# Two count matrices written in the order of the edges, the attention weights of layer 1 as the larger of 1 and a product

## The chip, the cores and the metric

The kernel runs on one core of a Trainium2 chip. Its engines are TensorE (PE, with its weight loads shown as PEld), VectorE (DVE), ScalarE (ACT), GpSimd (POOL) and SyncE (SP, which here only issues transfers). Six runs of the kernel before took 5446.58 to 5467.45 us, median 5455.3 us. The time is the device time of one execution in microseconds; lower is better.

## The reference, cut to what matters

A graph of N = 3125 nodes with 256 features and E = 50000 edges, sorted by `dst`, goes through four graph layers, each followed by a sum with its input and a layer norm. Layer 0 is a two-stage attention with a feed-forward part, layer 1 an attention with four heads, layer 2 two convolutions that sum over the edges and back, layer 3 a message product. The change is about layer 1 and about two matrices that layers 1 and 2 read:

```python
x  = h @ W                      # 3125 x 64
el = x @ Wl.T; er = x @ Wr.T    # 3125 x 4 heads
e  = exp(leaky_relu(el[src] + er[dst], 0.2))
w  = e / max(segment_sum(e, src), 1e-12)[src]
out[head] = segment_sum(w[:, head] * x[dst], src)
```

The kernel does not gather for layer 1. It writes a dense matrix `mats[0]`, in which row `dst`, column `src` holds how many edges lead from `src` to `dst`, and goes through all pairs: weight of a pair = count times exp(leaky_relu(el + er)). With the slope 0.2, exp(leaky_relu(z)) = exp(0.2 z) * exp(0.8 max(z, 0)); the factor exp(0.2 z) splits into a factor of the source and one of the target and is taken outside. `mats[1]` is the same matrix with rows and columns exchanged. Layer 2 reads both.

## The kernel before, in words

Nodes are padded to NP = 3200 = 25 tiles of 128 (`NN` = 25), edges to 50048 = 391 columns of 128 (`NT` = 391). The input `src` and `dst` come as 128 x 391 arrays whose column j holds the edges 128 j to 128 j + 127.

**Preparation** (`prepare`, L1991). The first projection, the query, key and value rows of layer 0, and the weights of layer 3's edges (`edge_weights`, L1890). `counts` (L1061) finds for each edge how many of the next edges are the same pair (`more`) and whether the same pair came before (`seen`); it works with partition p holding the edges 391 p to 391 p + 390, from an earlier copy of the edges in memory. It makes `count` (what is to be written), `put0` and `put1` (where in `mats[0]` and `mats[1]`); an edge whose pair came before, or a padding edge, is sent to a place behind the matrix. `put_by` and `fetch_by` carry such arrays through memory past a branch that chooses the path for sorted edges.

**Layer 0** (`attend`, L1405, called for l = 0 and l = 1) goes tile by tile over 25 tiles of 128 target nodes. Each tile's edges lie in a run of S = 17 columns of 128 slots. GpSimd gathers the key and value rows of the 17 columns with 17 indirect transfers (`fetch`, in three parts of 6, 6 and 5), then one more (`mine`) for the row sums' maxima. TensorE makes scores and sums, and the feed-forward of a group of three tiles (`feed`, L1302) is pumped in between. In `attend` every GpSimd and SyncE instruction is kept in program order (`InOrder`, L981). GpSimd's order in a tile is: 6 gathers of the next tile, fills, `mine`, then the next tile's other 11 gathers.

**Fills.** One fill is an indirect transfer of 128 counts of 2 bytes to 128 places of a matrix. `fill` (L1126) places it after a given transfer of GpSimd; L1487 puts FILL = 11 fills of `mats[0]` into each of the 25 tiles of l = 0, and L1620 the remaining 116 behind the last tile of l = 0. The fills of one matrix are declared independent of each other; a reader of the matrix waits for all of them. Cleared rows of `mats[1]` are also written in l = 0.

**Layer 1** (`layer1`, L1683). Three column blocks of 1280, 1280 and 640 sources (RS = 1280), each in two halves of two heads, each with 25 steps, one per tile of targets: 150 steps. A step loads a 128 x 1280 piece `m` of `mats[0]` (L1742, four buffers). For each of two heads it makes relu(el + er) (three times in five on VectorE, L1749, else on ScalarE, L1747), its exponential on ScalarE (L1751), the product with the counts on VectorE (L1752), and multiplies it into `acc` on TensorE (L1755). Each of the first 131 steps ends with `fill_slowly` (L1136): SyncE loads 3 columns of `put1` into a small tile (L1139, two buffers), and GpSimd makes three fills of `mats[1]` (L1142). SyncE's queue is strictly in order: the load of `put` for a step waits until a buffer is free, and the `m` of a later step stands behind it.

**Layers 2 and 3** read both matrices by blocks (`conv`, L1789), then gather rows of 1 KB (L91) for the last layer.

Of the kernel before, what the change touches and what calls it, by code (L numbers as in the profile page):

```python
# [57 lines left out]
FILL, FILL1 = 11, 3  # L58
# [943 lines left out]
class Sorted(General):  # L1002
# [58 lines left out]
    def counts(self, k, cp, sp, raw):  # L1061
# [6 lines left out]
        self.put1 = self.dram.tile([P, NT], I32, name="put1d")  # L1068
# [24 lines left out]
        nc.vector.tensor_copy(self.count, more)  # L1093
        d, src, code = (v[:, HALO:HALO + NT] for v in (d, src, code))
# [4 lines left out]
        nc.vector.tensor_max(away, away, pad)  # L1099
        behind = cp.tile([P, NT], F32, name="behind")  # L1100
        nc.gpsimd.iota(behind, pattern=[[1, NT]], base=NP * NP, channel_multiplier=NT,
                       allow_small_or_imprecise_dtypes=True)
        back = cp.tile([P, NT], F32, name="back")
        nc.vector.scalar_tensor_tensor(back, src, float(NP), d, op0=ALU.mult, op1=ALU.add)
        put1 = cp.tile([P, NT], I32, name="put1s")
        for c, to in ((code, self.put0), (back, put1)):
            gap = sp.tile([P, NT], F32, name="gap")
            nc.vector.tensor_sub(gap, behind, c)
            nc.vector.tensor_mul(gap, gap, away)
            nc.vector.tensor_add(to, gap, c)  # L1110
        nc.sync.dma_start(self.put1, put1)
# [8 lines left out]
    def zeros(self):  # L1120
        z = self.keep.tile([P, ZB], BF16, name="zmat")
        self.nc.vector.memset(z, 0.0)
        self.mats = [self.dram.tile([NP * NP + EP, 1], BF16, name=f"mat{i}") for i in range(2)]
        return z

    def fill(self, i, put, j, behind):  # L1126
# [6 lines left out]
        tc.declare_no_dep(ins.ins, group=f"fill{i}", reason="each place is written once")  # L1133
        tc.add_to_no_dep_group(f"fill{i}", ins.ins)

    def fill_slowly(self, i, sp, j0, j1):  # L1136

        put = sp.tile([P, FILL1], I32, name="put1")
        ins = self.nc.sync.dma_start(put[:, :j1 - j0], self.put1[:, j0:j1])  # L1139
        self.tc.keep_in_program_order(ins)  # L1140
        for j in range(j0, j1):
            ins = self.nc.gpsimd.indirect_dma_start(  # L1142
                out=self.mats[i], out_offset=bass.IndirectOffsetOnAxis(ap=put[:, j - j0:j - j0 + 1], axis=0),
                in_=self.count[:, j:j + 1], in_offset=None)
            self.tc.declare_no_dep(ins.ins, group=f"fill{i}", reason="each place is written once")
            self.tc.add_to_no_dep_group(f"fill{i}", ins.ins)
# [258 lines left out]
    def attend(self, l, qw):  # L1405
# [6 lines left out]
        with ExitStack() as at:  # L1412
# [48 lines left out]
            def scores(t):  # L1461
# [25 lines left out]
                for c in range(t * FILL, (t + 1) * FILL if l == 0 else 0):  # L1487
# [100 lines left out]
            for t in range(NN + 2):  # L1588
# [31 lines left out]
                for c in range(NN * FILL, NT if l == 0 and t == NN else 0):  # L1620
# [62 lines left out]
    def layer1(self, parts):  # L1683

        nc, tc, a = self.nc, self.tc, self.a
        A1 = D1 + 1
        mat = self.mats[0][:NP * NP, :].rearrange("(d s) o -> d (s o)", s=NP)
        with ExitStack() as at:  # L1690
# [14 lines left out]
            nc.vector.tensor_copy(wlb, l1.wr[:, H1:, None].to_broadcast([D1, H1, P]))  # L1705
            nc.scalar.activation(fe, er, AF.Exp, scale=0.2)
# [5 lines left out]
            def scores(s0, h0):  # L1712

                el = lp.tile([P, 2, RS], F32, name="el")
                for h in range(2):
                    for c in range(s0, min(s0 + RS, NP), 512):
# [3 lines left out]
                        nc.scalar.copy(el[:, h, c - s0:c - s0 + n], e_p[:, :n])  # L1720
# [4 lines left out]
            fills = iter(range(0, NT, FILL1))  # L1725
            for s0 in range(0, NP, RS):
                R = min(RS, NP - s0)
                ot = op.tile([A1, H1, RS], F32, name="ot")
                for h0 in range(0, H1, 2):
# [6 lines left out]
                    for t in range(NN):  # L1736
# [5 lines left out]
                        nc.sync.dma_start(m[:, :R], mat[t * P:(t + 1) * P, s0:s0 + R])  # L1742
                        for h in (h0, h0 + 1):
                            e = ep.tile([P, RS], F32, name="e")
                            z = er[:, t, h:h + 1]
                            if (2 * t + h) % 5 in (1, 3):
                                nc.scalar.activation(e[:, :R], el[:, h - h0, :R], AF.Relu, bias=z)  # L1747
                            else:
                                nc.vector.tensor_scalar(e[:, :R], el[:, h - h0, :R], z, 0.0,  # L1749
                                                        op0=ALU.add, op1=ALU.max)  # L1750
                            nc.scalar.activation(e[:, :R], e[:, :R], AF.Exp, scale=0.8)  # L1751
# [461 lines left out]
```

## Time and profile before

| | |
|---|---|
| median of six runs | 5455.3 us |
| profiled execution, its time / its span | 5455.55 us / 5453.7 us |
| busy: PE / DVE / ACT / POOL | 3957.5 / 2731.3 / 1436.7 / 2241.3 us |
| preparation | 0 to 285 us |
| layer 0, l = 0 | 285 to about 1873 us |
| layer 0, l = 1 | about 1873 to 2922 us |
| layer 1 | 2922 to 3613 us |
| layer 2 | 3613 to 4523 us |
| layer 3 | 4523 to 5454 us |
| fills in l = 0 (L1130) | 391, mean 976 ns |
| fills in layer 1 (L1142) | 391, mean 1252 ns |

The profile is of one execution. A busy time is the time in which an engine had an instruction under way; what lies between is idle time, put down to what ended it. "issue" is time in which the engine waited for nothing that the profile shows, "remote" a wait ended by something that it can't name. In a windows view each row is a stretch of the span in microseconds, its length, then for each engine the busy time and in brackets how many instructions began there, then the granted TensorE clock (1.00 is full), the share of the DMA engines and GB/s.

### The profile page before, as it was taken

How to read it: one execution, taken by the hardware profiler on the slowest of the kernel's cores; microseconds unless marked ns; L12 is line 12 of the kernel's file. 1: busy time of each engine (PE TensorE's matmuls, PEld its weight loads, DVE VectorE, ACT ScalarE, POOL GpSimd, SP SyncE). 2: the span in 40 equal slices, each digit the busy share in tenths (PEclk: the TensorE clock that was granted, in tenths of full speed). 3: DMA queues.
4: the chain of work that ended last, by engine and by line, in shares of the span. 5: the costliest groups of instructions: out<-in, count | busy, mean ns of one | idle time of the engine just before them, and what ended most of it. 6: DMA issues, size and time to landing. Idle time of an engine off the chain costs nothing.

```text
span 5453.7 us, 54504 instructions
## 1 busy us (share of the span) xinstructions
PE 3957.5 (73%) x18909; PEld 2660.9 (49%) x18909; DVE 2731.3 (50%) x5301; ACT 1436.7 (26%) x2460; POOL 2241.3 (41%) x2116
## 2 busy tenths in 40 slices
PE   6843656555555357777779989789999994777787
PEld 3432434344343245555564333346556553766677
DVE  7934535454453156666665888751221232444444
ACT  4600112111111002221225787765211110000000
POOL 0055544545456454454434878610000005455552
PEclk8866867777777668887888999899999996888878
DMA  8554534444330254555433222123333332122221
GB/s 192 145 180 120 151 106 134 137 132 138 100 115 21 93 162 147 154 168 146 146 118 81 68 61 68 41 76 89 92 104 87 100 111 76 58 68 68 70 70 38
DMA packets 381015, 577.19 MB, mean 106 GB/s; under 512 B 104265, under 2 KB 284100, under 8 KB 380669
## 3 DMA queue, kind: packets, MB, share of 16 engines
q1 hardware_dynamic: 264906, 286.55, 19.2%
q0 software_dynamic: 115824, 287.06, 18.1%
q8 instruction: 152, 2.49, 0.2%
q14 instruction: 133, 1.09, 0.1%
HBM read 486.46 MB, written 86.91 MB: 105 GB/s over the span
## 4 chain that ended last, share of the span: by engine, by line
PE 45%; another core or an unknown queue 17%; DVE 13%; issue 7%; POOL 5%; DMA 3%; ACT 2%; SPq 0%; DVEq 0%; ACTq 0%; POOLq 0%
PE cv L1806 9%; PE acc L1967 5%; PE acc L1547 5%; PE cv L1808 4%; PE acc L1755 4%; PE acc L1964 4%; PE qe L1471 3%; PE mm L1329 3%; POOL mat L1142 2%; PE mm L1343 2%; POOL kv L995 2%; DVE ws L1962 2%; DVE kv L1545 1%; DVE oh L1047 1%
## 5 line engine op out<-in xcount | busy, mean ns | idle before, releaser
L995 POOL DMA_INDIRECT kv<-kv,k_src x850 | 855.8, 1007 | 771.2 <-issue 232.7
L91 POOL DMA_INDIRECT g<-l_tab,k_src x425 | 445.6, 1048 | 1363.3 <-issue 1089.3
L1471 PE MATMUL qe<-q,oht 128*128 128x256 bf16 x2550 | 425.1, 317 | 550.0 <-DVE kv L1473 379.2
L1473 DVE TENSOR_TENSOR kv<-kv,qe 128x512 f32<-128x512 f32 (+1 forms) x450 | 289.3, 654 | 806.8 <-remote 509.8
L1471 PEld LDWEIGHTS <-oht 128*128 128x128 bf16 x2550 | 331.0, 148 | 655.5 <-issue 580.6
L1755 PE MATMUL acc<-e,xe 128*65 128x512 f32 (+2 forms) x1600 | 577.6, 517 | 67.0 <-DVE e L1752 45.3
L1142 POOL DMA_INDIRECT mat<-k_count,put x391 | 489.5, 1252 | 245.3 <-DMA put<-put1d 130.5
L1962 DVE TENSOR_TENSOR ws<-oh,w_n 128x512 f32<-128x512 f32 x425 | 290.4, 691 | 430.7 <-PE acc L1967 277.7
L1964 PE MATMUL acc<-g,ws 128*128 128x256 f32 x850 | 319.6, 463 | 216.6 <-DVE ws L1962 161.5
L1547 PE MATMUL acc<-kv,oh 128*128 128x264 f32 x1700 | 434.7, 413 | 33.5 <-DVE kv L1545 32.6
L1130 POOL DMA_INDIRECT mat<-k_count,k_put x391 | 381.5, 976 | 119.1 <-issue 119.1
L1967 PEld LDWEIGHTS acc<-g,ws 128*128 128x128 f32 x2550 | 411.0, 220 | 34.1
L1755 PEld LDWEIGHTS acc<-e,xe 128*65 128x65 f32 x1600 | 215.5, 142 | 421.9 <-issue 315.2
L1806 PE MATMUL cv<-parts,m 128*128 128x512 bf16 x1250 | 413.0, 381 | 7.5 <-DMA m<-mat 7.2
L1806 PE MATMUL cv<-mids,m 128*128 128x512 bf16 x1250 | 408.4, 379 | 10.7 <-DVE y L1828 9.5
L1967 PE MATMUL acc<-g,ws 128*128 128x128 f32 x2550 | 406.8, 303 | 0.0
L1547 PEld LDWEIGHTS acc<-kv,oh 128*128 128x128 f32 x1700 | 343.3, 206 | 109.9 <-DVE kv L1545 45.1
L1752 DVE TENSOR_TENSOR e<-e,m 128x1280 f32<-128x1280 f32 (+1 forms) x300 | 369.4, 1264 | 46.8 <-DMA m<-mat 25.5
L1806 PEld LDWEIGHTS <-m 128*128 128x128 bf16 x2500 | 245.0, 98 | 295.0 <-DMA m<-mat 9.3
L1808 PE MATMUL cv<-parts,m 128*128 128x256 bf16 x1250 | 339.2, 274 | 0.0
L1808 PE MATMUL cv<-mids,m 128*128 128x256 bf16 x1250 | 338.8, 273 | 0.0
L1751 ACT ACTIVATE e<-e 128x1280 f32<-128x1280 f32 (+1 forms) x300 | 317.5, 1087 | 66.0 <-DVE e L1749 47.7
(285 smaller groups left out, 5696.5 us busy)
## 6 DMA issues: line engine op xcount, KB each, us to landing
m<-mat SPq DMA_DIRECT2D x550, 160.0 KB
mat<-zmat SPq DMA_DIRECT2D x40, 1000.0 KB
m<-mat SPq DMA_DIRECT2D x100, 320.0 KB
keys<-e_dst SPq DMA_DIRECT2D x50, 544.0 KB
q<-q SPq DMA_DIRECT2D x100, 192.0 KB
kv<-kv,k_src POOLq DMA_INDIRECT x850
kv<-qkv SPq DMA_DIRECT2D x50, 256.0 KB
g<-l_tab,k_src POOLq DMA_INDIRECT x425
```

The lines of the kernel that those rows point to most:

```text
L91: return self.nc.gpsimd.indirect_dma_start(out=out, out_offset=None, in_=table, in_offset=bass.IndirectOffsetOnAxis(ap=idx, axis=0))
L995: ins = of(*args, **kw)
L1130: ins = tc.nc.gpsimd.indirect_dma_start(out=self.mats[i], out_offset=bass.IndirectOffsetOnAxis(ap=put, axis=0), in_=self.count[:, j:j + 1] ...
L1142: ins = self.nc.gpsimd.indirect_dma_start(out=self.mats[i], out_offset=bass.IndirectOffsetOnAxis(ap=put[:, j - j0:j - j0 + 1], axis=0), in ...
L1471: nc.tensor.matmul(qe[:, u, :], s.slots[:, h0 + s0 + u, :], s.q[:, k, :], start=(k == 0), stop=(k == 2))
L1547: nc.tensor.matmul(s.acc, s.oh[i][:, u, :], kv[:, u, D:], start=(h0 + u == 0), stop=(h0 + u == S - 1))
L1755: nc.tensor.matmul(accs[h, c][:, :n], xe[:, t, h, :], e[:, c:c + n], start=(t == 0), stop=(t == NN - 1))
L1806: nc.tensor.matmul(accs[i], block, parts[:, b, :2, :].rearrange("p a f -> p (a f)"), start=(b == 0), stop=False)
L1808: nc.tensor.matmul(accs[i][:, :D], block, parts[:, b, 2, :], start=False, stop=(b == NN - 1))
L1962: nc.vector.tensor_tensor(ws, oh[:, s, None, :].to_broadcast([P, 4, P]), w4[:, t, s, :, None].to_broadcast([P, 4, P]), op=ALU.mult)
L1964: nc.tensor.matmul(acc0, ws[:, 0, :], g[:, s, :], start=(s == 0), stop=(s == S - 1))
L1967: nc.tensor.matmul(acc1[:, m], ws[:, 1 + m, :], gb[:, 0:m + 2:m + 1, :], start=(s == 0 and m == 0), stop=(s == S - 1 and m == 2))
```

## The change

**Edge order.** `counts` now ends by writing one array `numbers` to memory: the count for an edge that is the first of its pair and real, else zero. A new function `places`, called after `edge_weights`, reads it back so that column j holds the edges 128 j to 128 j + 127 (four transposes on TensorE), loads `dst` and `src` as they come in, and makes `put0` and `put1` in that order; both also go to memory (`puts`). An edge with a zero count is sent behind the matrix.

**Exact dependences.** Since edges are sorted by target and 17 columns hold all edges of a tile's run, rows t of `mats[0]` are complete when its fills 0 to 17 (t + 1) - 1 have come. `filled` declares readers and fills independent of each other, and `row_of_counts` gives the load of `m` in step t of the first 25 steps just these fills to wait for.

**Where the fills go.** `mats[0]`: 3 in each tile of l = 0 and 50 behind its last tile, 2 in each tile of l = 1 and 130 behind its last tile (305 in all), and the last 86 in layer 1, 6 per step. `mats[1]`: 391 in layer 1 after them, 5 per step. There are 15 + 79 = 94 steps with fills.

**Weights.** With z = el + er, exp(0.8 max(z, 0)) = max(1, exp(0.8 el) exp(0.8 er)) = 1 + relu(exp(0.8 el) exp(0.8 er) - 1). `el` is stored as its exponential already (the copy from PSUM becomes an Exp), `fr` holds the target's factor, both shifted by `mid` to keep them in range. A step's head is then one ScalarE instruction (relu of factor times `el` minus 1) and one VectorE instruction (plus 1, times counts).

```diff
-FILL, FILL1 = 11, 3
+FILL = 3, 2
+FILLED = 0, 125, 305
+FILL0, FILL1 = 6, 5
...
-        nc.vector.tensor_copy(self.count, more)
...
+        nc.vector.tensor_mul(away, away, more)
+        nc.vector.tensor_sub(pad, more, away)
+        nc.sync.dma_start(self.numbers, pad)
+
+    def places(self, cp, rp):
+        n = cp.tile([P, LCH, P], F32, name="n_rows")
+        rows = self.numbers.rearrange("p j -> (p j)").rearrange("(r e) -> r e", e=P)
+        tp = rp.tile([P, 4, P], F32, name="rad_p")
+        for c in range(LCH):
+            m = min(P, NT - c * P)
+            nc.sync.dma_start(n[:m, c, :], rows[c * P:c * P + m, :])
+            nc.tensor.transpose(tp[:, c, :m], n[:m, c, :], self.ident[:m, :m])
+        num = tp.rearrange("p c e -> p (c e)")[:, :NT]
+        nc.vector.tensor_copy(self.count, num)
+        nc.vector.tensor_scalar(real, num, 0.0, None, op0=ALU.is_gt)
...
+        for (u, v), to in ((ends, self.put0), (ends[::-1], put1)):
+            gap = cp.tile([P, NT], F32, name="gap")
+            nc.vector.scalar_tensor_tensor(gap, u, float(NP), v, op0=ALU.mult, op1=ALU.add)
+            nc.vector.tensor_sub(gap, gap, behind)
+            nc.vector.tensor_mul(gap, gap, real)
+            nc.vector.tensor_add(to, gap, behind)
+        nc.sync.dma_start(self.puts[0], self.put0)
+        nc.sync.dma_start(self.puts[1], put1)
...
+    def filled(self, i, ins):
+        for g in (f"fill{i}", f"read{i}"):
+            self.tc.declare_no_dep(ins, group=g, reason="each place is written once")
+        self.tc.add_to_no_dep_group(f"fill{i}", ins)
+        self.fills[i].append(ins)
+
+    def row_of_counts(self, t, ins):
+        self.tc.declare_no_dep(ins, group="fill0", keep=self.fills[0][:S * (t + 1)],
+                               reason="the edges of this row have come")
...
-                for c in range(t * FILL, (t + 1) * FILL if l == 0 else 0):
+                for c in range(FILLED[l] + t * FILL[l], FILLED[l] + (t + 1) * FILL[l]):
                     self.fill(0, self.put0[:, c:c + 1], c, behind)
...
-                for c in range(NN * FILL, NT if l == 0 and t == NN else 0):
+                for c in range(FILLED[l] + NN * FILL[l], FILLED[l + 1] if t == NN else 0):
                     self.fill(0, self.put0[:, c:c + 1], c, behind_all[0])
...
-                        nc.scalar.copy(el[:, h, c - s0:c - s0 + n], e_p[:, :n])
+                        nc.scalar.activation(el[:, h, c - s0:c - s0 + n], e_p[:, :n], AF.Exp, scale=0.8,
+                                             bias=low[:, h0 + h:h0 + h + 1])
...
-            fills = iter(range(0, NT, FILL1))
+            fills = [(0, j, FILL0) for j in range(FILLED[2], NT, FILL0)] + [(1, j, FILL1) for j in range(0, NT, FILL1)]
+            fills = iter(fills)
...
-                        nc.sync.dma_start(m[:, :R], mat[t * P:(t + 1) * P, s0:s0 + R])
+                        ins = nc.sync.dma_start(m[:, :R], mat[t * P:(t + 1) * P, s0:s0 + R])
+                        if s0 == h0 == 0:
+                            self.row_of_counts(t, ins.ins)
                         for h in (h0, h0 + 1):
                             e = ep.tile([P, RS], F32, name="e")
-                            z = er[:, t, h:h + 1]
-                            if (2 * t + h) % 5 in (1, 3):
-                                nc.scalar.activation(e[:, :R], el[:, h - h0, :R], AF.Relu, bias=z)
-                            else:
-                                nc.vector.tensor_scalar(e[:, :R], el[:, h - h0, :R], z, 0.0,
-                                                        op0=ALU.add, op1=ALU.max)
-                            nc.scalar.activation(e[:, :R], e[:, :R], AF.Exp, scale=0.8)
-                            nc.vector.tensor_mul(e[:, :R], e[:, :R], m[:, :R])
+                            nc.scalar.activation(e[:, :R], el[:, h - h0, :R], AF.Relu, scale=fr[:, t, h:h + 1],
+                                                 bias=ones)
+                            nc.vector.scalar_tensor_tensor(e[:, :R], e[:, :R], 1.0, m[:, :R],
+                                                           op0=ALU.add, op1=ALU.mult)
...
-                        j = next(fills, None)
-                        if j is not None:
-                            self.fill_slowly(1, sp, j, min(j + FILL1, NT))
+                        for i, j, n in islice(fills, 1):
+                            self.fill_slowly(i, sp, j, min(j + n, NT))
...
             self.edge_weights(cp, rs, rp, *ew)
+            self.places(cp, rp)
             self.put_by()
```

Before the first step of layer 1 the changed kernel also finds `mid`, 0.4 times the difference between the largest `el` and the largest `er` of each head: a maximum over nodes, a transpose, another maximum, a small product on TensorE and four Exp instructions for `fr` (`fr`, `mid`, `low` in `layer1`). `fill_slowly` is as before, but loads from `puts[i]` a tile of up to six columns.

## Prediction

> **What bounds the kernel now.** I read the stages by windows, then the waits within a stage, then single instructions. No engine is busy throughout, so each stage has its own limit. The first two rows are the tile loops of layer 0, l = 0 and l = 1 (24 tiles between the first and the last `mine`), the next two are what follows the last `mine` in each.
>
> ```profile
> 339.50:1669.10 1329.60, 716.82 (x3400) 530.50 (x3399) 629.69 (x1223) 217.62 (x398) 685.02 (x690) 0.72 0.44 126
> 1919.90:2834.80 914.90, 645.05 (x3338) 506.39 (x3336) 591.04 (x1136) 189.90 (x351) 445.81 (x426) 0.81 0.52 154
> 1669.10:1873.00 203.90, 86.81 (x294) 57.74 (x293) 44.60 (x104) 29.17 (x64) 117.29 (x117) 0.71 0.07 19
> 2834.80:2927.20 92.40, 79.08 (x316) 57.11 (x316) 37.38 (x88) 32.96 (x70) 0.94 (x1) 0.82 0.20 53
> ```
>
> A tile takes 1329.6/24 = 55.4 us with 11 fills and 914.9/24 = 38.1 us without. In both, TensorE and VectorE do about the same work: 3.0 us more of TensorE and 1.6 us more of VectorE per tile at l = 0. The tails differ in the same way, 203.9 with 116 fills against 92.4 us. So fills cost time here though nothing in the tile loop reads them. The timeline shows how: VectorE stands for 65 and 41 us on a sum from TensorE, and GpSimd, done with its fills, waits another 51 us for the rows that this work makes.
>
> ```profile
> 1789.65 0.42 DVE L1347 TENSOR_TENSOR hs<-hs,mm 128x256 f32<-128x256 f32 x1 [65.38 <-remote]
> ...
> 1831.64 0.42 DVE L1347 TENSOR_TENSOR hs<-hs,mm 128x256 f32<-128x256 f32 x1 [40.90 <-remote]
> ```
> ```profile
> 1820.85 0.95 POOL L1130 DMA_INDIRECT mat<-k_count,k_put  x1 [0.30 <-issue]
> 1873.10 0.99 POOL L995 DMA_INDIRECT kv<-kv,k_src  x1 [51.29 <-DMA kv<-qkv]
> ```
>
> Why TensorE is slow beside a run of fills the profile does not say; I use the price only.
>
> Layer 1 is another matter. There fills run beside a TensorE that is nearly always busy (118.15 of 120 us, clock 1.00):
>
> ```profile
> 3300.00:3420.00 120.00, 118.15 (x330) 44.13 (x327) 101.88 (x86) 95.40 (x86) 96.53 (x75) 1.00 0.28 70
> 3480.00:3571.00 91.00, 66.78 (x225) 27.93 (x224) 57.12 (x85) 54.81 (x78) 69.71 (x64) 0.95 0.21 50
> ```
>
> The first row is 25 full steps with 75 fills: 4.8 us a step. A fill there takes 96.53/75 = 1.29 us and 0.30 us pass before the next, so three need 4.76 us: GpSimd is as full as TensorE. The second row is half-size steps: 64 fills of 1.09 us, again GpSimd's pace. After the last fill the half-size steps are shorter: 53 products, 26.5 steps, in 91 us (3.4 us a step) before, 32 products in some 40 us (2.5 us) after:
>
> ```profile
> 3480.00:3571.00 91.00, 42.67 (x53) 0.95 0.21 50
> 3571.00:3613.60 42.60, 25.27 (x32) 0.94 0.26 73
> ```
>
> The groups of layer 1 (count, busy, mean ns; then the idle time before):
>
> ```profile
> L1142 POOL DMA_INDIRECT mat<-k_count,put x391 | 489.5, 1252 | 245.3 <-DMA put<-put1d 130.5 <-issue 114.8
> L1752 DVE TENSOR_TENSOR e<-e,m 128x1280 f32<-128x1280 f32 x200 | 289.4, 1485 | 17.8 <-issue 9.0 <-ACT e L1751 5.7 <-DMA m<-mat 2.7
> L1751 ACT ACTIVATE e<-e 128x1280 f32<-128x1280 f32 x200 | 246.5, 1264 | 30.9 <-DVE e L1749 18.5 <-issue 11.3
> ...
> L1747 ACT ACTIVATE e<-el,er 128x1280 f32<-128x1280 f32 x80 | 108.5, 1356 | 57.0 <-PE acc L1755 54.9 <-issue 2.1
> L1749 DVE TENSOR_SCALAR e<-el,er 128x1280 f32<-128x1280 f32 x120 | 106.9, 892 | 57.2 <-PE acc L1755 55.2 <-issue 1.2
> ```
>
> A fill spreads from 0.96 to over 1.8 us, by what VectorE does meanwhile:
>
> ```profile
> 3330.00 1.80 POOL L1142 DMA_INDIRECT mat<-k_count,put  x1 [0.30 <-issue]
> ```
> ```profile
> 3329.49 4.29 DVE L1752 TENSOR_TENSOR e<-e,m 128x1280 f32<-128x1280 f32 x3
> ```
>
> **The change, part by part.** The sum is made against the profiled execution, 5455.55 us, 1.85 us over its span and 0.25 us from the median.
>
> *Preparation, +5 us.* Eight VectorE operations over 391 columns (one of before took 559 ns) now stand behind the product that ends the edge weights, some 5 us, and the arrays go to memory after them; the loads of `numbers`, `dst`, `src` lie beside the long run of edge weights. Bounds 0 (hidden by the transposes there) and +15 (two more waits on memory, like the 5.11 us for `k_key` at the stage's end).
>
> *Tile loops of layer 0, -204 us.* Eight fills fewer in each of 25 tiles, two more in each of 25: 150 fewer. Of the 17.3 us between the tiles some 2.3 are other work, so 15.0/11 = 1.36 us a fill. Bounds: 1.26 us (a fill's own 0.96 + 0.30) and 17.3/11 = 1.57: -189 to -236, if a short burst costs in proportion.
>
> *Tail of l = 0, -76 us.* 50 fills instead of 116. In proportion to 111.5/116 = 0.96 us it is -64; if the rows come 51 us after a burst of 50 x 1.3 = 65 us, 116 instead of 204 us, it is -88. I take the middle.
>
> *Tail of l = 1 and layer 1, +243 us.* From the last `mine` (2834.9) to the end of layer 1 (3613.6) took 779 us. GpSimd now has 130 + 86 + 391 = 607 fills there, in one chain. First the 130: 116 took 1670.5 to 1821.8, 1.305 us each, so 170 us. SyncE loads the first `put` of layer 1 only behind the last stores of the feed-forward, which by the first tail come 51 us after the burst (221 us), and if TensorE is not held, soon after it (175 us). I weigh them three to one: 208 us.
>
> Then 477 fills. SyncE must wait for a buffer before each `put`, and the `m` of two steps later stands behind it; so the steps go at GpSimd's pace: five fills a step. ScalarE drops from about 3.6 to 2 x 1.356 = 2.7 us per full step and VectorE from 4.0 to 2 x 1.485 = 3.0 us (a two-operation product of 128x256 took 414 ns, the plain one 417), but TensorE's 4.3 to 4.7 us stay, and five fills need 6.3 us even at 1.26 each. A fill: 1.26 us with VectorE idle, 1.39 with VectorE 63% busy (3480 to 3571), 1.59 at 85% (3300 to 3420). VectorE will be busy 3.0 of 6.8 us, 44%; between the first two rows that is 1.36. 477 x 1.36 = 649 us; bounds 601 and 737 (layer 1's mean of before, 1.252 + 114.8/391 = 1.545).
>
> Last, the final `put` lets the load of step 95 go; 55 steps follow without fills: 5 x 4.5 + 15 for the change of block + 50 x 2.5 + a load = 165 us. 208 + 649 + 165 = 1022, less 779. The new small operations before step 0 and the waits on exact rows lie inside: row 17 needs the first group of layer 1, and its load already stands behind later groups. If GpSimd were not the limit, the small operations would cost some 6 us.
>
> The Trainium skill speaks against moving fills here: "SBUF — State Buffer", section "Who interferes with whom", has VectorE in its two-port mode, and in reads with two inputs, shut GpSimd out of a shared port. It infers that two-input products leave descriptor writing alone; the removed `tensor_scalar` would then be the whole trouble, a fill would fall to 1.26 us and the result to 5376 us. The 1.80 us fill inside three two-input products contradicts the inference, so I keep 1.36.
>
> *Sum:* 5455.6 + 5 - 204 - 76 + 243 = 5424 us.
>
> **Rivals.**
>
> 1. *GpSimd stays as slow in layer 1 as before; slower.* Place: the 477 fills. For it: VectorE still makes two long two-input products a step, and 75 fills beside them took 1.59 us apiece. Against: VectorE's share of time halves. At 1.545 us it is +88, 5512 us. It decides from 1.45 us a fill on: 477 x 0.09 = 43 us brings 5467, the edge of slower.
> 2. *Short bursts hide.* GpSimd waited 18.3 us for `scores` before the last `mine` of l = 0, so three or two fills could fit. Tiles of l = 0 would fall to 38.1 + 2.3 and l = 1 stay: -375 instead of -204, 5253 us. Against: 11 fills would then have fitted in part as well, and cost more than their own length.
> 3. *A burst has a fixed price,* half of the 15 us. Then l = 0 gains 25 x 8 x 0.68 = 136 and l = 1 loses 25 x (7.5 + 1.4) = 222: 5714 us. Against: nothing shows a restart apart from the length.
> 4. *Layer 1 takes the fills easily:* 1.26 us, no held tail, 175 + 601 + 165 = 941: +162, 5343 us.
> 5. *TensorE cools down.* Waiting a third of each step, it falls to a clock of 0.5, as in the first tail: 8.8 us a full step, 95 x 2.0 = 190 us more, 5614 us. Against: at 73% busy from 3480 to 3571 it kept 0.95.
>
> **How the numbers follow.** Chances: my forecast 0.48, rival 1 0.28, rival 2 0.10, rival 4 0.06, rivals 3 and 5 0.04 each. A measurement tells about 0.2%, 11 us, from no change. The forecast's own range is 5375 to 5470: 0.40 of it faster, 0.07 within, 0.01 slower; rival 1 gives 0.01 within and 0.27 slower. Faster 0.40 + 0.10 + 0.06 = 0.56, same 0.08, slower 0.36. The range reaches down between rivals 2 and 4 and up past rival 1 at its dearest row (1.59 us: 5534): 5285 to 5560.
>
> **What would show it.** Tiles of 43 to 45 us at l = 0 and 40 to 42 at l = 1; some 205 us from the last `mine` to the first fill by L1184; a fill in layer 1 of 1.03 to 1.10 us; VectorE at about 44% in the full steps and TensorE at two thirds, waiting on `e`, which waits on `m`; then 165 us without fills. The forecast is wrong if layer 1's fills are over 1.15 us long, if l = 1 tiles grow by over 5 us, or if the granted clock in layer 1 falls to 0.7.

## The result, and the profile after

The changed kernel takes 5504.85 us (median of 20 runs, 5477.55 to 5550.34), the kernel before 5456.31 us beside it. The ratio is 1.0094 (95% interval 1.0078 to 1.0111): slower by 0.9%, where 0.6% faster was forecast. The profiled execution took 5506.15 us, its span 5504.4 us; the table compares it with the profiled execution of before.

| stretch | before, us | after, us | change | forecast |
|---|---|---|---|---|
| start to the first `mine` | 339.6 | 332.7 | -6.9 | +5 |
| 24 tiles of l = 0 | 1329.5 | 1089.0 | -240.5 | the two: |
| 24 tiles of l = 1 | 914.8 | 983.7 | +68.9 | -204 |
| last `mine` of l = 0 to the first of l = 1 | 250.9 | 178.3 | -72.6 | -76 |
| last `mine` of l = 1 to layer 2 | 778.8 | 1082.6 | +303.8 | +243 |
| layers 2 and 3 | 1840.1 | 1838.0 | -2.1 | 0 |
| sum | | | +50.6 | -32 |

The experiments were run in six sets of two kinds, in which the kernel before itself took 5460 to 5518 us (sets 1, 3 and 4; 5456 us in the runs above, which belong to this first kind) or 4482 to 4486 us (sets 2, 5 and 6, the second kind), so every kernel is compared with the kernel before of its own set.

The windows of the changed kernel, in the columns explained earlier. The first two rows are the tile loops, the next two what follows the last `mine` in each, then 120 us of full steps of layer 1 and the part of layer 1 behind the last fill.

```profile
332.70:1421.70 1089.00, 700.10 (x3400) 526.40 (x3399) 628.92 (x1223) 217.25 (x398) 504.27 (x498) 0.78 0.53 153
1421.70:1600.00 178.30, 102.69 (x382) 70.74 (x382) 58.99 (x126) 29.29 (x64) 78.07 (x76) 0.71 0.25 81
1600.00:2583.80 983.80, 654.99 (x3338) 511.30 (x3336) 591.53 (x1137) 189.78 (x351) 486.55 (x475) 0.79 0.49 143
2583.80:2802.50 218.70, 85.43 (x316) 60.72 (x317) 37.26 (x94) 35.10 (x74) 130.72 (x131) 0.63 0.10 22
...
2960.00:3080.00 120.00, 83.06 (x206) 28.65 (x205) 49.19 (x34) 52.16 (x41) 94.70 (x84) 0.94 0.19 45
...
3510.00:3663.00 153.00, 140.59 (x497) 62.33 (x496) 124.21 (x258) 127.91 (x170) 0.00 (x0) 0.94 0.21 56
```

Layer 0 took 244 us less, where 280 was forecast. In layer 1 the steps go at GpSimd's pace: 84 fills, 94.70 us busy, in 120 us, so 1.127 us a fill and 0.30 us before the next, 1.43 us each and 7.1 us for the five of a step. TensorE is busy 69% of that time, VectorE 41%. The groups (count, busy, mean ns; then the idle time before):

```profile
L1184 POOL DMA_INDIRECT mat<-k_count,put x477 | 550.6, 1154 | 201.6 <-issue 140.2
...
L1816 DVE SCALAR_TENSOR_TENSOR e<-e,m 128x1280 f32<-128x1280 f32 (+1 forms) x300 | 373.2, 1265 | 386.9 <-DMA m<-mat 290.8
...
L1814 ACT ACTIVATE e<-el,l_one,fr 128x1280 f32<-128x1280 f32 (+1 forms) x300 | 381.2, 1275 | 374.5 <-PE acc L1820 244.6
```

The product now waits for `m`, 290.8 us in all, and `m` is late because SyncE's queue stands at the loads of `put` (L1181), which wait for a fill to free a buffer. From 2960 to 3500 us (what waits, for what; us, times, longest):

```profile
SPq L1181 <- DMA mat<-k_count,put: 263.0, 79, 7.2
```
```profile
DVE e L1816 <- DMA m<-mat: 242.7, 57, 5.9
```

The l = 1 tail is held as the one of l = 0 was: the 130 fills end at 2755.1 us, and the first of layer 1 comes 47.47 us later.

```profile
2802.59 2.22 POOL L1184 DMA_INDIRECT mat<-k_count,put  x1 [47.47 <-DMA put<-put0d]
```

From the last `mine` to that fill it is 218.8 us, the 477 fills take 704.7 us to the end of the last, and 159.1 us follow.

### The profile page after: what moved, and what is told of

Its sections match the earlier page's. It is cut to its first block, busy times and chain, and to the rows that moved or that the text cites. A ratio compares the mean times of both kernels' runs of the same rounds, so it can differ in the third digit from the quotient of the medians.

```text
span 5504.4 us, 54269 instructions
## 1 busy us (share of the span) xinstructions
PE 4002.7 (73%) x18916; PEld 2674.4 (49%) x18916; DVE 2614.9 (48%) x5135; ACT 1365.5 (25%) x2338; POOL 2222.8 (40%) x2116
## 4 chain that ended last, share of the span: by engine, by line
PE 45%; another core or an unknown queue 14%; DVE 12%; issue 9%; POOL 8%; DMA 2%; ACT 2%; SPq 0%; ACTq 0%; DVEq 0%; POOLq 0%
PE cv L1870 9%; POOL mat L1184 8%; PE acc L2031 5%; PE acc L1588 5%; PE cv L1872 4%; PE qe L1512 4%; PE acc L2028 4%; PE mm L1370 3%; PE mm L1384 2%; PE acc L1820 2%; DVE ws L2026 2%; DVE kv L1586 1%; DVE kv L1514 1%; DVE oh L1050 1%
## 5 line engine op out<-in xcount | busy, mean ns | idle before, releaser
L1820 PE MATMUL acc<-e,xe 128*65 128x512 f32 (+2 forms) x1600 | 625.4, 549 | 187.9 <-DVE e L1816 129.2
L1184 POOL DMA_INDIRECT mat<-k_count,put x477 | 550.6, 1154 | 201.6 <-issue 140.2
L1816 DVE SCALAR_TENSOR_TENSOR e<-e,m 128x1280 f32<-128x1280 f32 (+1 forms) x300 | 373.2, 1265 | 386.9 <-DMA m<-mat 290.8
L1814 ACT ACTIVATE e<-el,l_one,fr 128x1280 f32<-128x1280 f32 (+1 forms) x300 | 381.2, 1275 | 374.5 <-PE acc L1820 244.6
L1159 POOL DMA_INDIRECT mat<-k_count,k_put x305 | 304.9, 1000 | 93.9 <-issue 93.9
```

Of the source, the lines that this page charges most:

```text
L1184: ins = self.nc.gpsimd.indirect_dma_start(out=self.mats[i], out_offset=bass.IndirectOffsetOnAxis(ap=put[:, j - j0:j - j0 + 1], axis=0), in ...
L1814: nc.scalar.activation(e[:, :R], el[:, h - h0, :R], AF.Relu, scale=fr[:, t, h:h + 1], bias=ones)
L1820: nc.tensor.matmul(accs[h, c][:, :n], xe[:, t, h, :], e[:, c:c + n], start=(t == 0), stop=(t == NN - 1))
```

## Experiments

**One half of the change at a time (set 1, before 5459.8 us).** The first kernel has the new weights alone, the second the new order and places of the fills alone:

```diff
 # e1, against the kernel before
...
-                            nc.scalar.activation(e[:, :R], e[:, :R], AF.Exp, scale=0.8)
-                            nc.vector.tensor_mul(e[:, :R], e[:, :R], m[:, :R])
+                            nc.scalar.activation(e[:, :R], el[:, h - h0, :R], AF.Relu, scale=fr[:, t, h:h + 1],
+                                                 bias=ones)
+                            nc.vector.scalar_tensor_tensor(e[:, :R], e[:, :R], 1.0, m[:, :R],
+                                                           op0=ALU.add, op1=ALU.mult)
 # e2, against the changed kernel: the same lines the other way round
```

> The kernel before with the new weights alone (fills as before: 11 per tile of l = 0, three per step of layer 1). My theory now: layer 1 goes at GpSimd's pace, and a fill is stretched by the two-input product, which stays (2 x 1.485 us a step); the removed single-input operation hardly mattered. Then a full step stays at 4.6 to 4.8 us, a fill at 1.2 to 1.3 us, and the time at 5425 to 5460 us, 0 to 30 us below before. Rival, that the removed operation stretched the fills: 1.1 us a fill, TensorE's pace of 4.3 us a step, 45 to 70 us below before, 5385 to 5410 us.

> The changed kernel with the old weights: edge order, exact dependences and the new places of the fills alone. My theory: 477 fills set layer 1 whatever the weights cost, some 7.1 to 7.5 us per full step, the first fill of layer 1 to the last 700 to 740 us; 5500 to 5540 us, so this half alone makes the kernel slower by 0.9 to 1.5%. Rival, that the weights matter for the fills: 1.25 us busy a fill as before, 7.8 us a step, 740 us or more, 5545 to 5580 us.

The weights alone: 5464.97 us, 1.001 of before (0.9988 to 1.0032), no difference. Layer 1 from its first product to layer 2 took 671 us instead of 680, a fill 1.273 us instead of 1.252: taking 180 one-input operations (120 of them over 1280 elements) from VectorE did not shorten the fills. The fills alone: 5545.05 us, 1.014 (1.010 to 1.0179). That is 40 us more than the whole change takes (the two intervals still overlap), five above the range I gave and the lowest value of the rival: 477 fills took 734 us, 1.227 us busy each. So the loss comes with the fills. The weights give some of it back: by the traces 29 us in the fills and 15 us in the steps behind the last one (174 against 159 us).

**What stretches a fill, and what the steps cost without fills (set 2, before 4482.4 us).** These three kernels leave out or replace a part of the work, so that only their times count; each was run once.

```diff
 # e3b, against the changed kernel
-                            nc.vector.scalar_tensor_tensor(e[:, :R], e[:, :R], 1.0, m[:, :R],
+                            nc.vector.scalar_tensor_tensor(e[:, :1], e[:, :1], 1.0, m[:, :1],
 # e4b, as e3b with this line ahead
+                            nc.vector.tensor_scalar(e[:, :R], e[:, :R], 1.0, 0.0, op0=ALU.add, op1=ALU.max)
 # e5, against the changed kernel
-            fills = [(0, j, FILL0) for j in range(FILLED[2], NT, FILL0)] + [(1, j, FILL1) for j in range(0, NT, FILL1)]
+            fills = [(0, j, FILL0) for j in range(FILLED[2], NT, FILL0)]
```

> The changed kernel without VectorE's product in layer 1 (only the first column of each piece is still multiplied by its counts, the rest of the counts is left out; TensorE takes ScalarE's output). If the product stretches the fills: a fill of layer 1 at 0.96 us plus 0.30, five in 6.3 us, first fill to last 605 us instead of 705, 5400 to 5415 us. If ScalarE, TensorE or the transfers stretch them: fills stay at 1.13 us and the time near 5500.

> The changed kernel with a one-input operation of VectorE in the place of the product (counts left out but for the first column): 892 ns for 128x1280, as the removed one of before. If VectorE's busy time stretches a fill whatever the operation: 60% of the stretch stays, 1.07 us a fill, first to last 660 us, 5455 to 5470 us. If one-input operations shut GpSimd out more than two-input ones, as the Trainium skill's page "SBUF — State Buffer" (section "Who interferes with whom") infers: 1.13 us or more and 5500 or more. If only the second input matters: 0.96 us, 605 us, 5400 to 5415.

> The changed kernel without the 391 fills of the second matrix (it stays empty, layers 2's sums come out wrong): what layer 1 costs when GpSimd doesn't set its pace. Theory, that the fills alone set the pace: 15 steps at 8.5 us, then 85 steps at TensorE's 4.3 to 4.7 us and 50 at 2.2; from the last gather of layer 0 to the end of layer 1 some 840 us instead of 1083, 5250 to 5275 us. Rival, that TensorE or ScalarE has become slow in itself: over 5 us a full step, 5310 or more.

The times (4436.7, 4487.8 and 4320.8 us) belong to another kind of set than the expectations were written for; the fills can be compared with the changed kernel's in set 6, which took 1.134 us each and 690 us from the first to the end of the last. Without the product:

```profile
L1184 POOL DMA_INDIRECT mat<-k_count,put x477 | 459.0, 962 | 150.3 <-issue 141.5 <-DMA put<-put1d 8.8
```

With a one-input operation in its place:

```profile
L1184 POOL DMA_INDIRECT mat<-k_count,put x477 | 502.7, 1054 | 149.6 <-issue 142.1 <-DMA put<-put1d 7.2 <-DMA put<-put0d 0.3
...
L1816 DVE TENSOR_SCALAR e<-e 128x1280 f32<-128x1280 f32 (+1 forms) x300 | 216.9, 725 | 63.7 <-ACT e L1814 62.8
```

The 477 fills took 609 us (605 expected) and 652 us (660). So in set 2 the product alone makes the difference between 0.96 and 1.13 us, and what ScalarE, TensorE and the transfers add is below 0.01 us. A one-input operation stretches too: per microsecond of overlap a fill grew by some 0.35 us beside it and by 0.37 to 0.41 us beside the product (what the fills that met the operation took beyond 0.958 us, divided by their overlap, instruction by instruction; one-input in this kernel, the product in the changed one in both kinds of sets). The Trainium skill infers in "SBUF — State Buffer", section "Who interferes with whom", that two-input products leave descriptor writing alone. A fill, which has its places and counts as inputs besides, is stretched by them all the same; whether its reads or its writing is held up, these runs don't show.

Without the second matrix's fills, layer 1's full steps are 4.3 us, and TensorE has no pause:

```profile
2300.00:2360.00 60.00, 60.00 (x166) 22.87 (x165) 38.06 (x26) 40.87 (x32) 0.00 (x0) 1.00 0.26 71
```

So nothing but the fills makes a step 7.1 us long. From the last `mine` to layer 2 it is 826 us, where 840 was expected.

**Fills beside layer 2 (sets 2, 3 and 5).** The edge order completes the second matrix column by column, so layer 2's first pass can wait for a block of columns only. `f1` keeps 332 fills in layer 1 (five a step, then three) and puts 145 beside that pass; `f2` 300 (five, then two, then one) and 177, six for every third piece; `f3` is `f2` with the old weights; `h4` has two for every piece.

```diff
+    def columns_of_counts(self, c, ins):
+        n = min(NT, 5 * S * (c + 1))
+        self.tc.declare_no_dep(ins, group="fill1", keep=self.fills[1][:n],
+                               reason="the edges of these columns have come")
...
-                nc.sync.dma_start(m, mat[b * P:(b + 1) * P, c * CT * P:(c + 1) * CT * P])
+                ins = nc.sync.dma_start(m, mat[b * P:(b + 1) * P, c * CT * P:(c + 1) * CT * P])
+                if fills is not None:
+                    self.columns_of_counts(c, ins.ins)
+                    for j in islice(fills, 1 if (c * NN + b) % 3 == 0 else 0):
+                        self.fill_slowly(1, sp, j, min(j + FILL2, NT))
```

> The edge order used once more: columns of the second matrix are complete in order too, so layer 2's first pass over it waits, block of columns by block of columns, only for the fills of these. Layer 1 keeps 86 fills (five a step) and 246 (three a step); the other 145 go beside layer 2's first pass, where GpSimd has nothing to do. If fills cost only where GpSimd sets the pace: layer 1 falls by some 230 us, layer 2 stays at 927 us, 5260 to 5300 us in all. If fills slow layer 2's transfers or TensorE as they slow layer 0: up to 145 x 1.3 = 190 us come back there, 5450 to 5490 us.

> As the kernel that moved fills into layer 2, but so that GpSimd sets the pace nowhere: in layer 1 five fills a step for 18 steps, then two per full step and one per half step, the other 177 in layer 2's first pass, six for every third piece. If only GpSimd's pace costs: steps of 4.3 us in layer 1 after the first 18, layer 2 back at 903 to 910 us, 0.960 to 0.970 of before. If fills slow layer 2 by being there: layer 2 at 960 us or more and 0.98 or above.

> The same with the old weights. If TensorE sets the pace once GpSimd does not: the weights are worth 0 to 20 us (0.0 to 0.4%), full steps of 4.3 to 4.7 us with either. If the old weights cost for themselves: 40 us or more above the kernel with the new ones, as between the two with all fills in layer 1 (5545 against 5505).

> The kernel with spread fills, but in layer 2 two fills beside every piece instead of six beside every third: the same number at the same mean rate, in runs of 2.5 us with a pause of a microsecond behind each. If TensorE loses time only after some 10 us of unbroken fills: layer 2 falls from 1064 us to 930 us, 0.975 to 0.985 of before. If every fill takes its 0.77 us from layer 2: 1064 us again and 1.00.

> The changed kernel itself beside the others, since the kernel before took 5460 us in one set of runs and 4482 us in another. If layer 1 is what makes it slower: 1.005 to 1.015 of before in either kind of set, with layer 1 as long as in the first profile (705 us from the first to the last fill).

> The kernel before, for a trace of it under the conditions of this set. If fills lie on GpSimd's own chain in layer 0 in either kind of set: a tile of l = 0 takes 9 to 13 us longer than in the changed kernel, 8 fills fewer there; if short bursts hide when gathers wait less: under 4 us.

`f1` took 4427.62 us, 0.987 of before (0.9844 to 0.9895). In set 3 (before 5505.5 us) the changed kernel again took 1.0109 (1.0067 to 1.0152), `f2` 5508.26 us, 1.0011 (0.9982 to 1.004), `f3` 5539.56 us, 1.0065 (1.0041 to 1.0089). `h4` took 4436.04 us beside 4486.2 (one run). Layer 1 did what was expected: with two fills per step the full steps are 4.3 us, the same as with none. Here `f2`, 334 products, 12 a step, in 120 us:

```profile
3000.00:3120.00 120.00, 120.00 (x334) 45.98 (x333) 79.52 (x54) 83.54 (x66) 99.09 (x57) 1.00 0.32 80
```

The old weights of `f3` cost 31 us, between the two values expected. Its full steps are as long (330 products in the same 120 us); 21 us lie in the third half block, the first behind a change of column block (149 instead of 128 us). The two stretches also show that VectorE's share does not set a fill's length: at 66% in `f2` a fill took 99.09/57 = 1.74 us, at 84% in `f3` 1.35 us.

But layer 2, from its first product to the first gather of layer 3 927 us before, took 1015 us in `f1`, 1064 in `f2` and 1032 in `h4`: 0.6 to 0.8 us came back per fill, and in `h4` with its pauses as well. `h4` does not decide whether only unbroken runs cost, though: it ran in the other kind of set than `f2`, and there something else holds layer 2, as the waits show below.

`b0`, one run of before in set 3, had 56.6 and 39.2 us per tile against 46.2 and 41.5 in the changed kernel: 10.5 us for eight fills, as the first theory had it, and 2.3 us for two, 1.3 and 1.15 us each, near the 1.25 and 1.43 of the first comparison.

Two different things hold layer 2. In sets 2 and 5 it is SyncE's queue again (142 us of waits for fills in `f1`, 2804 to 2995 us). The waits of `h4` beside the first pass, SyncE's and TensorE's:

```profile
SPq L1192 <- DMA mat<-k_count,put: 194.7, 100, 6.3
```
```profile
PE cv L1886 <- DMA m<-mat: 74.6, 8, 32.1
```

In set 3 SyncE hardly waits for fills, and most of TensorE's waits are "issue", with nothing outstanding that the profile shows. The waits of `f2`:

```profile
PE cv L1885 <- issue: 32.4, 29, 2.5
PE cv L1883 <- issue: 22.4, 24, 2.5
```
```profile
SPq L1189 <- DMA mat<-k_count,put: 5.2, 3, 3.8
```

**Fills without any tie to SyncE (set 4, before 5517.5 us).** The second matrix's places stay in a tile of their own, and behind the last `mine` GpSimd has 216 and 391 fills with no wait between them. `g3` is the same with the old weights.

```diff
+        self.put1 = k.tile([P, NT], I32, name="put1k")
+        nc.sync.dma_start(self.put1, self.puts[1])
...
+    def fill_now(self, i, put, j):
+
+        self.fill(i, put[:, j:j + 1], j, self.behind)
...
+            for j in range(FILLED[2], NT):
+                self.fill_now(0, self.put0, j)
+            for j in range(NT):
+                self.fill_now(1, self.put1, j)
```

> The changed kernel with the places of the second matrix kept in a tile of their own (391 words per partition), so that no fill waits for SyncE and no load of SyncE for a fill: behind the last gather of layer 0 GpSimd makes 216 fills of the first and 391 of the second matrix without a stop. Rows of the first and blocks of columns of the second matrix are waited for exactly. If layer 1 was slow because its steps were tied to GpSimd's pace through the loads of the places: steps at TensorE's 4.3 us from the 23rd on, layer 1 some 100 us shorter than in the kernel with spread fills, 30 to 90 fills left beside layer 2 (20 to 65 us there), 0.955 to 0.975 of before. If fills at GpSimd's full rate slow ScalarE, VectorE or TensorE themselves: steps stay over 5 us and the ratio at 0.99 or above.

> The same with the old weights. Theory: TensorE's 4.3 to 4.7 us a step hide them, but VectorE's 4.0 us a step instead of 3.0 stretch the fills (1.35 instead of 1.2 us), so that some 40 more fills fall beside layer 2: 20 to 50 us above the kernel with the new weights. Rival, that the weights cost nothing where steps are free of GpSimd: within 10 us.

`g2` took 5901 us, 1.0696 (1.0631 to 1.0762): its first theory missed by far, and its rival, that the fills slow the engines themselves, had the direction but nothing like the size. `g3` took 5946 us, 1.0775 (1.0701 to 1.0848). Its 45 us above `g2` lie in the range of its theory, but not for its reason, since the last fill ended 640 us before layer 2 began. The feed-forward behind the last `mine`, 92 us of work, took 677 us, as long as GpSimd needed for most of its 607 fills. Two windows of `g2`, one in that tail and one in the first steps of layer 1:

```profile
2900.00:3000.00 100.00, 6.08 (x16) 4.63 (x16) 2.91 (x8) 0.00 (x0) 78.35 (x72) 0.52 0.02 0
3312.00:3417.00 105.00, 26.16 (x36) 7.23 (x36) 8.95 (x6) 8.71 (x6) 81.43 (x76) 0.60 0.07 16
```

In the second, TensorE issued 36 products and 36 weight loads beside 76 fills, about one instruction per fill; in the first it was 32 beside 72. Once the fills were over, steps were 4.3 us. The tail of l = 0 in the kernel before looks the same late in its run of 116 fills:

```profile
1765.00:1830.00 65.00, 5.66 (x16) 4.34 (x16) 1.03 (x3) 0.00 (x0) 43.13 (x45) 0.55 0.02 2
```

Over that whole run it was 400 instructions, 3.4 per fill, so the hold is not there from the first fill on. That it is one cause in all three places is not shown.

**More tiles for the places (sets 5 and 6, before 4486 us).** The groups of five and six fills stay as in the changed kernel, but their `put` tiles are 40 instead of 2. `h1` and `i1` are this kernel, `i2` is the changed kernel, `i3` has 5 and 4 fills per tile of layer 0 instead of 3 and 2, with 30 instead of 50 behind l = 0 and 50 instead of 130 behind l = 1, and `h5` takes the fills out of layer 0's tiles (125 and 180 behind them) with two `put` tiles as in `f2`, three per full and two per half step and 45 beside layer 2.

```diff
 # h1, i1, i3 (with the exact waits of layer 2's first pass)
+            up = pool("l1u", 40)
...
-                            self.fill_slowly(i, sp, j, min(j + n, NT))
+                            self.fill_slowly(i, up, j, min(j + n, NT))
 # i3
-FILL = 3, 2
-FILLED = 0, 125, 305
+FILL = 5, 4
+FILLED = 0, 155, 305
 # h5
+FILL = 0, 0
```

> The changed kernel with 40 tiles for the places in layer 1 instead of 2 (groups of six and five fills as before, SyncE no longer waits for a fill before it loads the next places) and with exact waits of layer 2's first pass. If TensorE came to a standstill in the uncoupled kernel because the run of fills had no wait in it: here every group still begins with a wait, so layer 1's steps fall to 4.3 to 5 us and the time to 0.97 to 0.98 of before. If any run of fills without a pause holds TensorE to about one instruction per fill: a step, 24 instructions, takes over 10 us in layer 1, and the ratio is over 1.03.

> The cheapest places by what the runs priced: no fills in the tile loops of layer 0 (there 1.25 and 1.43 us each), 125 behind l = 0 and 180 behind l = 1 (0.8 to 1.1 us each), in layer 1 five a step for 18 steps, then three per full and two per half step, the last 45 in layer 2, one beside every second piece. Theory: tiles of 35 us at l = 0 and 38 at l = 1, layer 1's steps 4.8 us, layer 2 at 905 to 930 us; 0.975 to 0.99 of before. Rival, that fills cost the same wherever they stand once GpSimd or TensorE is in their way: 0.995 to 1.005.

> The kernel with 40 tiles for the places again, now timed with an interval. In a set of runs like the second (before at 4485 us): 0.965 to 0.970 of before, as in the single look. In a set like the first (before at 5460 to 5517 us) it tells two theories apart. If a wait at the head of each group keeps TensorE supplied: 0.965 to 0.98. If unbroken fills hold TensorE to an instruction per fill there, as in the uncoupled kernel: over 1.03.

> The changed kernel itself beside it. In a set like the second, where tiles of layer 0 took 32 and 30 us with few fills and with none: layer 1 as long as before it (705 us from the first fill to the last), 4520 to 4540 us, 1.008 to 1.013 of before; in a set like the first 1.007 to 1.013.

> The kernel with 40 tiles for the places, and 5 and 4 fills per tile of layer 0 instead of 3 and 2, so that 50 instead of 130 stand behind l = 1. If a few fills per tile hide where TensorE isn't held (second kind of set): tiles stay at 32 and 30 us, steps 16 to 22 of layer 1 no longer wait for rows (22 us a step), 90 to 110 us below the kernel with 40 tiles. If they do not hide (first kind of set, 1.25 and 1.43 us each): 134 us more in the tiles, some 80 less behind l = 1, 30 to 60 us above it.

| kernel | time, us | of before (95%) | last `mine` to layer 2 | layer 2 |
|---|---|---|---|---|
| `i2`, the changed kernel | 4520.79 | 1.0071 (1.0049 to 1.0092) | 1028 us | 927 us |
| `h5` | 4497.23 | 1.0022 (1.001 to 1.0034) | 932 us | 929 us |
| `i1` | 4335.74 | 0.966 (0.9633 to 0.9686) | 838 us | 928 us |
| `i3` | 4329.67 | 0.9639 (0.9614 to 0.9663) | 767 us | 927 us |

`h1`, one run of the kernel of `i1` in set 5, took 4336.94 us beside 4486.21.

`i1` does the same fills as `i2`, in the same groups, and the same work on every engine, but is 185 us faster, with 190 us less between the last `mine` and layer 2. It differs in two things, the 40 tiles and the exact waits, and no run has one without the other. The exact waits alone could save nothing: in `i2` the last fill ends 158 us before layer 2 begins. In `i1` it ends 108 us behind that point, so without them, as an estimate from these two traces, layer 2 would have begun 108 us later and 82 of the 190 us would be left. The waits of SyncE for fills, for `i2` (2300 to 2840 us) and then `i1` (2300 to 2790 us):

```profile
SPq L1181 <- DMA mat<-k_count,put: 460.1, 154, 7.5
```
```profile
SPq L1825 <- DVE e L1832: 263.9, 92, 8.6
SPq L1196 <- DMA mat<-k_count,put: 57.9, 17, 7.7
```

Windows of `i1`, a stretch of full steps and the start of layer 2:

```profile
2350.00:2460.00 110.00, 98.95 (x303) 38.09 (x302) 87.58 (x176) 84.88 (x96) 90.91 (x63) 1.00 0.23 58
...
2795.00:2903.00 108.00, 99.57 (x579) 61.10 (x592) 30.30 (x102) 72.62 (x181) 82.35 (x85) 0.95 0.35 92
```

GpSimd is as full as in the changed kernel, and a fill even longer (90.91/63 = 1.44 us, since VectorE is busier), but full steps are 4.3 us: `m` no longer waits for it. From its first product to layer 2 layer 1 took 747 us, against 937 in `i2` and 735 in `e5`, which leaves the second matrix's fills out. The 85 fills left over run beside layer 2 and cost it nothing. So in these sets the fills cost layer 1 their time through the tie, not for themselves. That only holds for the kind of set in which it ran; `i1` was not run in the other kind.

`i3` gained 6 us on `i1`, not the 90 to 110 expected: 71 us less behind the last `mine`, but its tiles grew from 32.1 to 33.8 and from 30.2 to 31.3 us. In these sets three and two fills per tile are free (`h5` has none and the same 32.1 and 30.2 us), two more cost 0.85 and 0.5 us each. `h5` missed its range, and came where its rival had it, for the same reason: it took away fills that cost nothing and lengthened the runs behind l = 0 (199 instead of 130 us from the last `mine` to the next) and l = 1.

## Why the prediction was wrong

*The step that failed: 477 fills at 1.36 us.* They took 704.7 us, 1.477 each, against 649: 56 of the 82 us between the forecast and the profiled execution. That alone turns the forecast of 32 us faster into 24 us slower. This is the place of rival 1, past its deciding point of 1.45, and the sign that the prediction named, fills over 1.15 us long, came narrowly (1.154). That the rival's time (5512 us) is nearly what came is in part luck: its fills were to cost 1.545 us, 88 us more, and the tile loops, 32 us worse than forecast, made up for what was missing. Three things that the step rests on were right: GpSimd's pace sets the steps, TensorE falls to two thirds (69%), VectorE to 44% (41%). Wrong was the price. I drew a line through rows by VectorE's share of the time and read 1.36 us at 44% (the line gives 1.35). Measured is 1.43 at 41%. The share is not what stretches a fill. What counts is the overlap with VectorE's operation: alone a fill takes 0.958 us, wholly beside the product 1.60 (some 75 of them), 0.41 us more per microsecond of overlap. A fill met the product for 0.47 us on average, and 0.958 + 0.30 + 0.47 x 0.41 = 1.45 us, which would have put the forecast at the edge of slower. The remaining 0.03 us is in the main idle time of GpSimd: three waits for `put`, 10 us in all. The overlap itself was measured afterwards; nothing in the prediction gives it.

*The weights' part in the fills.* I had taken the removed one-input operations for part of the fill's trouble. `e1` shows no shorter fills with them gone, and `e2` 0.07 us longer ones with them present at five fills a step, 29 us over the 477.

*Tile loops and tails.* -171.6 instead of -204: l = 0 gained 1.25 us a fill, not 1.36, in the 24 tiles between the rows (the first tile's fills lie before them); l = 1 lost 1.43 us a fill. Its tiles took 41.0 us, as forecast, those of l = 0 45.4 instead of 43 to 45. The tail of l = 0 came as forecast (-72.6). That of l = 1 is held as in the dearer of the two cases that I weighed (218.8 against 221 us), so weighing cost 11 us (three to one gives 209.5, not 208). The end without fills took 159 us (165).

*The preparation* can't be told apart: before the first `mine` lie also eight fills fewer, some 10 us at 1.25, so that -6.9 us fits the +5 forecast, but in six kernels of sets 1, 3 and 4 that are alike up to there it starts anywhere from 336.5 to 343.6 us.

*The other rivals.* A fixed price per burst (3) is out: two fills lengthened l = 1's tiles by 2.9 us, not 8.9. TensorE did not cool down (5): granted clock 0.80 to 0.94 in layer 1. Short bursts did not hide (2) and the tail was held (4) in the runs that the prediction is about. In set 6 they do hide and the tail is hardly held: tiles of 32.6 and 30.3 us, and the first fill of layer 1 180 us behind the last `mine` instead of 219. The changed kernel was still slower there, by 0.7%: its fills in layer 1 took 690 us.

*What I saw and did not follow.* The prediction says that `m` stands behind `put` in SyncE's queue and takes the pace as given. In set 6 the tie was itself the loss: with 40 `put` tiles and the exact waits of layer 2 the same fills cost 190 us less. Whether it would have been so in the runs that the prediction is about was not measured.

## What to carry to other kernels

Price an operation that another engine stretches by the microseconds in which the two overlap, from rows with that operation and rows without; a busy share mixes operations. When an in-order queue carries both the main loop's loads and those for a side job, two buffers make the main loop as slow as the side job: give the side job enough buffers to run behind, and let the readers of its results wait only for their part, before moving or trimming its work. Work moved off one bottleneck is only gained if its new place has slack for all of it; here, with two `put` tiles, a full step of layer 1 hid two fills (4.3 us), and the next three cost 0.9 us each (7.1 us).

## What the runs showed of the hardware

*Two kinds of sets.* The same kernel before took 5456 to 5518 us or 4482 to 4486 us (medians of sets). Layer 2 is alike in both (927 us in the changed kernel) and so are layer 1's steps of 4.3 us without fills. The difference lies where GpSimd gathers: the changed kernel's tiles of layer 0 took 45.4 and 41.0 us or 32.6 and 30.3 us, and its layer 3 took 910 or 611 us. Its mean granted clock was 0.83 or 0.91. What makes the difference was not found.

*TensorE beside a long run of fills.* In the first kind of set TensorE comes nearly to a standstill late in a long run of fills. Products and weight loads counted alike, it issued 32 instructions beside 45 fills in the tail of l = 0 before (row above), none beside the last 52 of the 130 fills of the tail of l = 1 in the changed kernel (2690 to 2755 us; 352 beside its first 39), and 32 to 104 beside 71 to 80 fills per 100 us in `g2` (2700 to 3200 us). In `g2` 354 of its 568 us of waits (2620 to 3290 us) are "issue"; the others end with VectorE or ScalarE, which had waited in turn. In the other kind the same tail of l = 1 shows no such hold. Here `i1`, 306 products and 305 loads beside 63 fills, 9.7 per fill:

```profile
1960.00:2045.00 85.00, 71.14 (x306) 52.82 (x305) 33.55 (x91) 29.99 (x65) 65.16 (x63) 0.86 0.18 43
```

Layer 1's groups of five did not hold TensorE in either kind (206 products beside 84 fills above), although these fills follow one another without a pause in time: in the changed kernel 473 of the 476 gaps between them are 0.3 us. Whether the waits that stand in the program between the groups or the lower need for instructions there is the reason stays open: the kernel with unbroken fills ran only in the first kind of set, the one with 40 `put` tiles only in the second.
